# A six-layer graph network on one core: the mask fetch in four parts, layer 1's sums made in two blocks, layer 2's queries begun earlier

## The chip, the core and the metric

The kernel runs on 1 core of one Trainium2 chip. The metric is the device time of one execution in microseconds, taken as the median of several runs. Engines are named as in the profile: PE multiplies matrices, DVE and ACT work element by element, POOL does a few small things, and SP only issues DMAs, one after the other in a fixed order.

## The reference, cut to what matters

There are 3327 nodes with 256 features and one adjacency matrix `adj`, which all layers share. Layers 0, 1 and 2 are three kinds of attention; layer 3 is a projection and three graph attention layers behind each other (called 3a, 3b, 3c). Each attention is masked by `adj`:

```python
# layer 1 (3a, 3b, 3c alike)
h = x @ W
e = h @ a[:D, 0][:, None] + (h @ a[D:, 0])[None, :]
e = where(e > 0, e, slope * e)
att = softmax(where(adj > 0, e, -1e12), axis=1)
x = layernorm(x + elu(att @ h))
# layer 2
scores = (x @ Wq.T + bq) @ (x @ Wk.T + bk).T / 16
x = layernorm(x + elu(softmax(where(adj > 0, scores, -9e15)) @ (x @ Wv.T + bv)))
```

Layer 0 is an attention by cosines of the same form.

## The kernel before, in words

Nodes are cut into 26 tiles of 128 (`NT`) and the columns of the attention into 7 blocks (`NB`), six of 512 columns and a last one of 256. The main loop (L1604) goes through steps (L, b, j): layer, block, tile. "Block 1/3" below means layer 1, block 3, and "position 18" in a block means that PE is at the products of tile 18.

**Weights.** `make(s)` builds the masked weights of a step some steps ahead of the products: 3 steps for layers 0 and 2, up to 7 for the others (L1625 to L1637). A weight is one ACT instruction (L788) and one DVE instruction (L801) that multiplies by the 0/1 mask. The mask of a block is one byte an element in SBUF, 26 slices of 512. Two mask buffers exist (`mpool`, L60). Layer 0 computes all masks and stores them to `mask_d` (L1145). From layer 1 on, the mask of the next block comes back by `fetch_mask` (L423): one DMA of 1664 KB, traced in step j = 8 (L1727).

**Products and sums.** Most blocks use a Strassen-like scheme (`products`, L915): for two tiles (a pair p, 13 pairs in a block) 7 products in place of 8, 28 matmul instructions of about 0.11 us. It needs sums of the value tiles (`combine`, L833: a small POOL memset, four DVE operations on 128x128 and a store of 256 KB to `t_d`), made once for each layer and pair, and fetched again for each block and pair (`fetch_tsum`, L863, 256.5 KB). Both take a buffer with the tag "tsum", of which there are 3: so the fetch for pair p can only be issued when PE has finished pair p - 3. Layer 1's first and last block (1/0 and 1/6) use plain products (L1700) and fetch nothing. Layer 1's twelve first sums were made in block 0/6 (pairs 0 to 2, steps 6, 12, 18), block 1/0 (pairs 3 to 8, steps 1, 5, ..., 21) and block 1/1 (pairs 9 to 11, steps 1, 5, 9).

**What sets the order.** Outside of its first steps the program is ordered by a planner: instructions are sorted onto their engines when their inputs and buffers are there in the planner's own estimate of the time; the order in which they are traced is their priority. So a DMA traced in step 8 may be placed on SP's queue far earlier. `tc.issue_after(ins)` ties an instruction behind another one on its engine. At run time each queue keeps the order that the planner gave it, so that what stands behind a waiting instruction starts late with it.

**Ends of blocks.** `finish` (L1079) joins a block's products, normalizes (L1163), turns tiles by a transposing DMA (`turn`, L1002, issued at L1009; copies to `pT` at L1020), projects (L1212), and in layer 1 writes the result rows back (`v<-o`, L1293), which wait for ACT (L1275). In block 1/6 the turned features of blocks 0 to 3 come back from DRAM (`turned_again`, L1023, copies at L1034), and `block2(0)` (L534) makes layer 2's first queries: eight matmuls (L541), two ACT instructions into `gT` (L548), a maximum on DVE (L556 to L561), a tiny matmul (L564) and a dozen tiny DVE operations up to `off` (L572). It was begun in step 14 (`begin`, L1741).

Of the kernel before, what the change touches and what calls it, by code (L numbers as in the profile page):

```python
# [33 lines left out]
def gnn_stack(ctx: ExitStack, tc: tile.TileContext, a: dict, N: int, out: bass.AP):  # L34
# [8 lines left out]
    nc = tc.nc  # L43
    NT = (N + P - 1) // P
    NP = NT * P
    NB = (NP + CH - 1) // CH
# [3 lines left out]
    def bw(b):  # L50
        return min(CH, NP - b * CH)
# [41 lines left out]
    for k in range(4):  # L93
# [5 lines left out]
    V = [  # L99
        [big.tile([P, D + 1], F32, name=f"v{i}_{t}") for t in range(NT)]  # L100
        for i in range(2)
    ]
# [5 lines left out]
    mask_d = [dram.tile([P, NT * bw(b)], U8, name=f"mask_d{b}") for b in range(NB)]  # L108
# [305 lines left out]
    masks = {}  # L414

    def new_mask(b):
        return mpool.tile([P, NT * CH], U8, tag="mask", name="mask")
# [2 lines left out]
        wd = bw(b)  # L420
        return masks[b][:, j * wd : (j + n) * wd]

    def fetch_mask(b):  # L423
        m = new_mask(b)
        nc.sync.dma_start(m[:, : NT * bw(b)], mask_d[b])
        return m

    adj_sum = {}
    stages = {}
# [403 lines left out]
    def combine(key, p, v, e=None):  # L833


        b1, b2 = v[2 * p], v[2 * p + 1]
        b11, b12, b21, b22 = b1[:, H:D], b1[:, :H], b2[:, H:D], b2[:, :H]
        if key == "2" and (key, p) not in kept:
            t = wts.tile([P, 4 * H], F32, tag=("w_l0_wqk", "row_1")[p % 2], name="tsum")
        elif (key, p) in kept or key in ("0", "1"):  # L840
            t = work.tile([P, 4 * H + 1], F32, tag="tsum", name="tsums", bufs=3)
        else:
            t = work.tile([P, 4 * H + 1], F32, tag="x4k", name="tsum", bufs=2)
        if (key, p) in kept:
            tsums[kept[key, p], p] = t
        t2, t3, t4, t1 = (t[:, c : c + H] for c in range(0, 4 * H, H))
        if e is None:
            if key != "2" or (key, p) in kept:
                nc.gpsimd.memset(t[:, 4 * H :], 1.0)
            nc.vector.tensor_tensor(t1, b12, b11, ALU.subtract)  # L850
            nc.vector.tensor_tensor(t3, b22, b12, ALU.subtract)
        else:
            one = t[:, 4 * H :]
            nc.vector.tensor_scalar(one, e[:, :1], 0.0, None, ALU.is_ge)
            nc.vector.scalar_tensor_tensor(t1, b12, one, b11, ALU.mult, ALU.subtract)
            nc.vector.scalar_tensor_tensor(t3, b22, one, b12, ALU.mult, ALU.subtract)
        nc.vector.tensor_tensor(t2, b22, t1, ALU.subtract)
        nc.vector.tensor_tensor(t4, t2, b21, ALU.subtract)
        nc.sync.dma_start(t_d[key][p][:, : t.shape[1]], t)

    fetched = [None]
# [742 lines left out]
    for s, (L, b, j) in enumerate(steps):  # L1604
        last = L.key == "3c"
# [118 lines left out]
        if L.key == "0" and b < NB - 1:  # L1724
            if j == 8:
                masks[b + 1] = new_mask(b + 1)
        elif j == 8 and not (last and b == NB - 1):  # L1727
            nb = (b + 1) % NB
            masks[nb] = fetch_mask(nb)
        if (b, j) == (1, 0):  # L1730

            if L.key == "3a":
# [5 lines left out]
        nl, nb = (L, b + 1)  # L1738
        if nb == NB:
            nl, nb = (None if last else layers[L.i + 1]), 0  # L1740
        begin = 14  # L1741
        if L.is_gat and b < NB - 1:
            begin = 2 if last and b == NB - 2 else 10
        if L.key == "0" and b == 3 and j < NT // 2 - 1:
            nc.sync.dma_start(t_d["2"][j][:, 4 * H :], ones[:, :1])
        if L.key == "0" and b == NB - 1 and j % 6 == 0 and 0 < j < 24:
            combine("1", j // 6 - 1, V[1])
        if L.key == "1" and j % 4 == 1 and j < (24, 12, 0, 0, 0, 0, 0)[b]:
            combine("1", (3 if b == 0 else 9) + j // 4, V[1])
        if L.key == "1" and b == NB - 1 and j > 0:  # L1750
            if j in (2, 4, 7, 10):
                again.append(turned_again(j // 3))
# [103 lines left out]
```

## Time and profile before

| | |
|---|---|
| median of 3 runs | 2266.18 us (2260.41 to 2271.84) |
| the profiled execution's own time | 2264.42 us |
| its span, first to last instruction | 2262.6 us |
| granted TensorE clock, mean | 0.996 |
| PE busy | 2221.0 us, 98% |
| DVE busy | 2022.4 us, 89% |
| ACT busy | 1368.2 us, 60% |
| mean DMA rate | 141 GB/s |

The profiled execution is one run; 1.82 us of its time lie outside of the span. With PE busy for 98%, a reader looks for the few places where PE has nothing to do, and compares blocks of one kind with each other: every block of layers 3a to 3c with 512 columns has the same products, and those without an interruption take 44.10 to 44.21 us.

### The profile page before, as it was taken

How to read it: one execution, taken by the hardware profiler on the slowest of the kernel's cores; microseconds unless marked ns; L12 is line 12 of the kernel's file. 1: busy time of each engine (PE TensorE's matmuls, PEld its weight loads, DVE VectorE, ACT ScalarE, POOL GpSimd, SP SyncE). 2: the span in 40 equal slices, each digit the busy share in tenths (PEclk: the TensorE clock that was granted, in tenths of full speed). 3: DMA queues.
4: the chain of work that ended last, by engine and by line, in shares of the span. 5: the costliest groups of instructions: out<-in, count | busy, mean ns of one | idle time of the engine just before them, and what ended most of it. 6: DMA issues, size and time to landing. Idle time of an engine off the chain costs nothing. (4 is left out here: it accounts for less than half of the span.)

```text
span 2262.6 us, 43919 instructions
## 1 busy us (share of the span) xinstructions
PE 2221.0 (98%) x16053; PEld 2035.4 (90%) x16053; DVE 2022.4 (89%) x5482; ACT 1368.2 (60%) x2317; POOL 87.9 (4%) x257
## 2 busy tenths in 40 slices
PE   9999999999999999999999999999999999999997
PEld 7788888889999789999999999999999999899997
DVE  7789999988989688998988889999899998899997
ACT  4677777775676645455454446666666765666663
POOL 0000001000000000000000000000000000000000
PEclk9999999999999999999999999999999999999999
DMA  8655655645765622233133254556545656355542
GB/s 278 197 167 181 194 191 192 191 133 162 178 171 144 195 52 78 67 82 92 48 96 81 66 145 153 152 152 163 140 123 152 152 149 163 101 165 161 152 121 57
DMA packets 218764, 318.84 MB, mean 141 GB/s; under 512 B 97597, under 2 KB 127028, under 8 KB 213940
## 3 DMA queue, kind: packets, MB, share of 16 engines
q1 hardware_dynamic: 209636, 307.90, 47.1%
q0 software_dynamic: 8640, 7.87, 2.4%
q8 instruction: 127, 2.08, 0.4%
q14 instruction: 89, 0.73, 0.1%
q10 hardware_dynamic: 272, 0.26, 0.0%
HBM read 243.97 MB, written 40.54 MB: 126 GB/s over the span
## 5 line engine op out<-in xcount | busy, mean ns | idle before, releaser
L788 ACT ACTIVATE re<-u,nrh,th 128x512 f32<-128x512 f32 (+1 forms) x728 | 531.0, 776 | 191.8 <-DVE ft L801 156.0
L947 PE MATMUL po<-tsums,qsum 128*128 128x128 f32 (+1 forms) x3240 | 451.9, 275 | 9.8 <-DMA tsums<-t_d 7.4
L801 DVE SCALAR_TENSOR_TENSOR ft<-re,rh,mask 128x512 f32<-128x512 f32 x598 | 433.3, 742 | 14.7 <-ACT re L788 13.0
L947 PEld LDWEIGHTS po<-tsums,qsum 128*128 128x128 f32 x3240 | 405.5, 192 | 12.2 <-DMA tsums<-t_d 6.0
L947 PE MATMUL po<-v,ft 128*128 128x129 f32 x2392 | 365.3, 275 | 0.7 <-DVE ft L801 0.6
L947 PE MATMUL po<-tsums,ssum 128*128 128x128 f32 (+1 forms) x2142 | 328.4, 276 | 8.5 <-DMA tsums<-t_d 3.2
L947 PEld LDWEIGHTS po<-v,ft 128*128 128x128 f32 x2392 | 321.4, 192 | 5.8 <-DVE ft L801 1.0
L947 PEld LDWEIGHTS po<-tsums,ssum 128*128 128x128 f32 x2142 | 296.4, 192 | 24.6 <-issue 5.0
L947 PEld LDWEIGHTS po<-v,e 128*128 128x128 f32 x1196 | 169.3, 191 | 35.6 <-issue 23.7
L1700 PE MATMUL po<-v,e 128*128 128x257 f32 x832 | 192.5, 382 | 0.8 <-DVE e L525 0.8
L524 ACT ACTIVATE ex<-ps,rq 128x512 f32<-128x512 f32 (+1 forms) x183 | 118.7, 652 | 112.0 <-PE ps L511 109.2
L1700 PEld LDWEIGHTS po<-v,e 128*128 128x128 f32 x832 | 156.3, 190 | 33.4 <-issue 9.7
L947 PE MATMUL po<-tsums,ft 128*128 128x128 f32 x1196 | 183.0, 275 | 0.0
L947 PE MATMUL po<-v,e 128*128 128x129 f32 x1196 | 182.3, 275 | 0.0
L511 PE MATMUL ps<-ft 128*128 128x512 f32 (+1 forms) x364 | 167.1, 564 | 0.4 <-ACT ex L524 0.4
L947 PE MATMUL po<-v,qsum 128*128 128x128 f32 x1080 | 164.9, 275 | 0.0
L947 PEld LDWEIGHTS po<-tsums,ft 128*128 128x128 f32 x1196 | 158.0, 192 | 0.2
L496 DVE SCALAR_TENSOR_TENSOR e<-ex,mask 128x512 f32<-128x512 f32 (+1 forms) x182 | 118.2, 651 | 42.2 <-ACT ex L676 16.5
L947 PEld LDWEIGHTS po<-v,qsum 128*128 128x128 f32 x1080 | 142.3, 192 | 0.0
L525 DVE SCALAR_TENSOR_TENSOR e<-ex,mask 128x512 f32<-128x512 f32 (+1 forms) x183 | 116.0, 642 | 28.4 <-ACT ex L524 27.9
L465 DVE CUSTOM_DVE_ANT_0 acc<-acc,stage 128x1024 uint16<-128x1024 uint16 (+1 forms) x168 | 108.5, 646 | 12.6 <-DMA stage<-in_adj_a 10.6
L649 PE MATMUL ps<-gsums,ksum 128*128 128x256 f32 x408 | 112.1, 382 | 0.7 <-ACT ex L660 0.7
(330 smaller groups left out, 3751.0 us busy)
## 6 DMA issues: line engine op xcount, KB each, us to landing
tsums<-t_d SPq DMA_DIRECT2D x217, 256.5 KB
mask<-mask_d SPq DMA_DIRECT2D x30, 1664.0 KB
stage<-in_adj_a SPq DMA_DIRECT2D x78, 512.0 KB
tsums<-t3a_d SPq DMA_DIRECT2D x77, 256.5 KB
tsums<-t3b_d SPq DMA_DIRECT2D x77, 256.5 KB
tsums<-t3c_d SPq DMA_DIRECT2D x77, 256.5 KB
mask_d<-mask SPq DMA_DIRECT2D x6, 1664.0 KB
xsum<-v POOLq DMA_DIRECT2D x60, 128.0 KB, 4.1
```

What stands on the lines that cost most here:

```text
L465: nc.vector.tensor_tensor(acc, acc, st[:, h * wd : (h + 1) * wd], ALU.add)
L496: last_masked[0] = nc.vector.scalar_tensor_tensor(e[:, :wd], t_[:, :wd], 0.0, mask(b, j), ALU.add, ALU.mult)
L511: nc.tensor.matmul(ps[:, :wd], FT[j // 4][:, 0, (j % 4) * P : (j % 4 + 1) * P], FT[b][:, 1, :wd], start=True, stop=True,)
L524: nc.scalar.activation(t_[:, c], ps[:, c], AF.Exp, scale=rq[:, j : j + 1])
L525: nc.vector.scalar_tensor_tensor(e[:, c], t_[:, c], 0.0, mask(b, j)[:, c], ALU.add, ALU.mult)
L649: nc.tensor.matmul(out, l, r, start=first, stop=True, skip_group_check=True)
L788: a_ = nc.scalar.activation(t_[:, :wd], self.u[b][:, :wd], AF.Relu, bias=self.nrh[:, j : j + 1], scale=self.th[:, j : j + 1],)
L801: v_ = nc.vector.scalar_tensor_tensor(e[:, :wd], t_[:, :wd], self.rh[:, j : j + 1], mask(b, j), ALU.add, ALU.mult,)
L947: nc.tensor.matmul(o, x, y, start=(p == 0 and g not in banks[:i]), stop=(p == NT // 2 - 1 and g not in banks[i + 1 :]),)
L1700: nc.tensor.matmul(pos[k], e[:, k * P : (k + 1) * P], V[L.i % 2][i], start=(i == 0), stop=(i == NT - 1),)
```

## The change

Three edits. The mask of the next block is fetched in four DMAs (tiles 0 to 7, 8 to 13, 14 to 19, 20 to 25), traced in steps 6, 8, 10 and 12, each tied on SP behind the last fetch of sums that has been traced by then. Layer 1's sums for pairs 0 to 7 are made in block 1/0 (steps 1, 4, ..., 22) and for pairs 8 to 11 in block 1/1 (steps 1, 3, 5, 7); none in block 0/6. In block 1/6, `block2(0)` is begun in step 11 in place of 14.

```diff
-    def fetch_mask(b):
-        m = new_mask(b)
-        nc.sync.dma_start(m[:, : NT * bw(b)], mask_d[b])
-        return m
+    PARTS = (0, 8, 14, 20, NT)
+
+    def fetch_mask(b, i):
+        c = slice(PARTS[i] * bw(b), PARTS[i + 1] * bw(b))
+        with tc.issue_after(fetched[0].ins):
+            nc.sync.dma_start(masks[b][:, c], mask_d[b][:, c])
...
-        elif j == 8 and not (last and b == NB - 1):
+        elif j in (6, 8, 10, 12) and not (last and b == NB - 1):
             nb = (b + 1) % NB
-            masks[nb] = fetch_mask(nb)
+            if j == 6:
+                masks[nb] = new_mask(nb)
+            fetch_mask(nb, j // 2 - 3)
...
+        if L.key == "1" and b == NB - 1:
+            begin = 11
...
-        if L.key == "0" and b == NB - 1 and j % 6 == 0 and 0 < j < 24:
-            combine("1", j // 6 - 1, V[1])
-        if L.key == "1" and j % 4 == 1 and j < (24, 12, 0, 0, 0, 0, 0)[b]:
-            combine("1", (3 if b == 0 else 9) + j // 4, V[1])
+        if L.key == "1" and b == 0 and j % 3 == 1 and j < 24:
+            combine("1", j // 3, V[1])
+        if L.key == "1" and b == 1 and j % 2 and j < 8:
+            combine("1", 8 + j // 2, V[1])
```

## The prediction

> **What bounds the kernel now.** I read the page's busy times first, then PE's waits by stretch, then a table of blocks, then the timelines of SP and PE around each wait. The page says that PE has almost no time to give away:
>
> ```profile
> PE 2221.0 (98%) x16053; PEld 2035.4 (90%) x16053; DVE 2022.4 (89%) x5482; ACT 1368.2 (60%) x2317; POOL 87.9 (4%) x257
> ```
>
> So the whole gain lies in 2262.6 - 2221.0 = 41.6 us, some 13 of them at the ends of the span. PE's waits, of the whole run (us in total, times, longest), show what the middle holds:
>
> ```profile
> PE po L947 <- DMA tsums<-t_d: 10.5, 8, 2.3
> PE pproj L1212 <- DVE pT L1020: 3.5, 4, 2.0
> PE po L947 <- DMA tsums<-t3b_d: 2.6, 4, 1.2
> ```
>
> The first row is all of layer 1. With the same rows of t3a_d (1.0) and t3c_d (0.9), fetched sums that come late cost 10.5 + 2.6 + 1.0 + 0.9 = 15.0 us. Now blocks against each other (stretch, length, busy times, granted clock, DMA share): 1/3, 1/4, 1/6, 3b/1, 3b/2.
>
> ```profile
> 606.81:656.34 49.53, 46.34 (x383) 45.44 (x381) 43.03 (x104) 31.12 (x46) 2.91 (x4) 0.97 0.74 182
> 656.34:700.44 44.10, 44.10 (x383) 43.69 (x381) 42.20 (x98) 29.96 (x45) 3.45 (x4) 1.00 0.64 156
> ...
> 750.21:791.76 41.55, 38.71 (x149) 28.61 (x148) 27.70 (x93) 30.23 (x47) 2.58 (x3) 0.96 0.61 173
> ...
> 1702.04:1747.73 45.69, 44.47 (x383) 43.84 (x382) 42.86 (x101) 28.99 (x45) 3.67 (x6) 1.00 0.62 159
> 1747.73:1791.94 44.21, 44.21 (x383) 43.77 (x382) 42.27 (x97) 29.36 (x45) 3.64 (x6) 1.00 0.61 159
> ```
>
> Equal work takes 44.1 us undisturbed and up to 49.5 us disturbed; DVE, at 42 to 43, is close behind. Block 1/3 loses 5.43 us, more than its waits, and its clock is 0.97: see below. What disturbs is seen on SP's and then PE's timeline of 3b/1:
>
> ```profile
> 1735.93 0.32 SPq L425 DMA_DIRECT2D mask<-mask_d  x1
> 1736.51 0.32 SPq L865 DMA_DIRECT2D tsums<-t3b_d  x1
> ```
> ```profile
> 1745.18 1.16 PE L947 MATMUL po<-tsums,ssum 128*128 128x128 f32 x8 [1.22 <-DMA tsums<-t3b_d]
> ```
>
> The mask fetch sits at position 18 to 20 of nearly every block, not where step 8 would put it: the planner has pulled it up to where its buffer comes free, and there SP waits for DVE's last masked weight of the block (in 3a/2 that ended at 1484.05, and the DMA went out at 1484.08). So it is fetched a block and a half ahead, in one piece, just before the fetches for the last pairs. In the trace's packets the mask issued at 736.67 moves from 737.63 to 742.78, and the fetch issued behind it at 737.10 has its first packet at 742.29: the pieces of one DMA stand in line before those of the next. The fetch at 1736.51 thus served PE 8.7 us later. A fetch is asked for when pair p - 3 is done, two pairs, 4 positions or about 6.3 us, ahead; a mask in front takes 5 of them. Two such waits in layer 1:
>
> ```profile
> 642.10 0.32 SPq L425 DMA_DIRECT2D mask<-mask_d  x1
> 646.81 2.03 SPq L1293 DMA_DIRECT2D v<-o  x2
> 648.95 0.53 SPq L865 DMA_DIRECT2D tsums<-t_d  x1
> ```
> ```profile
> 652.27 2.05 PE L947 MATMUL po<-tsums,ssum 128*128 128x128 f32 x8 [2.28 <-DMA tsums<-t_d]
> ...
> 744.97 1.61 PE L947 MATMUL po<-tsums,qsum 128*128 128x128 f32 x12 [1.85 <-DMA tsums<-t_d]
> ...
> 764.48 3.60 PE L1212 MATMUL pproj<-w_l_w,pT 128*128 128x256 f32 x8 [1.97 <-DVE pT L1020]
> ```
>
> **The change, part by part.**
>
> **Masks in layers 3a to 3c.** The ties put part i behind the fetch for pairs 6, 7, 8 and about 9 or 10 (step 6 looks 7 ahead, to tile 12), issued at positions 8 to 16, where SP has little else. The buffer has been free for half a block, so SP waits for nothing new. The first part lands some 8 positions before DVE needs it; the last, tiles 20 to 25, a block before. The parts for the first block of the next layer are tied only to the last fetch of block 5 and may still go together at position 20, but then behind it. I take the lengths above 44.21 (3a, 3b) and 44.10 (3c): 3b/1 1.48, 3b/3 0.48, 3b/5 1.02, 3c/1 1.16; and the bare waits of blocks that also lose elsewhere, 3a/0 0.45, 3a/2 0.57, 3b/0 0.42. Sum 5.6 us. Block 3a/0 has DVE busy for 44.96 of 45.48 us, so its share may stay: I count **-5.0**.
>
> **Masks in layer 1.** Late sums at the end of 1/2 (0.91), 1/3 and 1/5 (1.85) have a mask ahead. That of 1/3 costs more than its 2.28: the granted clock then stands at 0.5 for 3.41 us (652.07 to 655.48), 13 matmuls at 0.21 in place of 0.11. Block 1/3 lost 5.43, of which 0.51 and 0.40 are two waits at its start: 4.5 for this one. The Trainium skill, "TensorE: Matmul & The Clock Gate", Part 1, says that half clock follows an idle window of about 3.4 us; here 2.28 and 1.97 us sufficed, twice, while 2.06 at 705.63 did not. By the page the removal of this wait would be worth 2.3, by the rows 4.5. Sum 0.9 + 4.5 + 1.9 = 7.3. The result rows (L1293), which wait for ACT until 646.81, stay ahead of that fetch if the planner keeps its order; without the mask the fetch still has to leave at about 647.8 and be there at 650. I count **-6.0**. The waits at block starts (1.55 at 563.7; 0.99 and 2.06 after 701) follow a transposing DMA whose issue holds SP for 4.07 us at 699.30; they have no mask ahead, and I leave them.
>
> **Queries sooner.** In block 1/6 PE stands 1.97 us for pT, then runs eight projections at half clock (0.425 in place of 0.216, 1.67 lost), then 0.87 for L564: 4.5 us. The eight matmuls of L541 (3.44 us at 0.43 each) now come three steps sooner. They read FT of block 0, whose copies end at 759.70 in ACT's timeline, before PE stands still at 762.51. If they go in front of the projections, the wait is filled and the clock stays up. The `gT` buffer shares its tag with the transposed tiles still in flight until about 762, so ACT may hold it back: **-3.0**, ends 0 and -4.5. ACT's two instructions and DVE's maximum move with it into ACT's idle 2.54 us before 764.66.
>
> **Layer 1's sums.** A sum is 4 DVE operations of 0.28 us, a store, a buffer. Three leave block 0/6, where DVE is busy 32.48 of 35.57 us and PE waits 1.2 us for weights. But the trace has nine stores of sums from 428 to 469: the planner pulls them up wherever DVE seems free, whatever step traces them, and will again; I count 0 (ends 0 and -1.7). What does change is block 1/1: four sums in steps 1 to 7 in place of three in 1 to 9, through the 3 buffers that the fetches use. Walking through, pairs 4 to 6 get their buffers 2 positions (3.1 us) before need in place of 4, and a fetch takes 2 to 3 us. Today's 1/1 does as much without loss (44.10). I count **+1.5**; ends 0 and +8, if SP waits 2.8 us (25.0 over 9, SP's waits on L858 here) at each sum.
>
> **Price of the parts.** Three more issues of 0.32 us on SP for each of 35 masks, which is idle then; packets of 13312 B take 498 ns, of 4096 B 159 ns, of 2052 B 85 ns: one of 4096 B and three of 3072 B cost at worst, at the rate of the smallest, 540 ns, 8% or 0.4 us of 5 more on the ring. DVE waits at four slices in place of one, in its lead of 7 steps. **0**, ends 0 and +1.
>
> Sum -5.0 - 6.0 - 3.0 + 1.5 = -12.5: 2264.42 becomes 2251.9. The profiled run lies 1.76 below the median of 2266.18, so I say **2253** for the median.
>
> **The rivals.** 0.5% of the median, about what a measurement of this kernel can tell from no change, is 11.3 us; the forecast is just beyond it.
>
> *The queue's order, not the mask (22%).* If the result rows and transposing DMAs of layer 1 make its fetches late anyway, and the projections stay ahead of L541, only 5.0 and 0.9 of L564 remain, some -3 to -9: 2257 to 2263. For it speaks that 1/2 and 1/5 also wait where no mask is near.
>
> *More than the forecast (10%).* With the mask gone the planner sets the last two fetches ahead of the result rows; the block starts (4.6) and 0/6 go too: all ends together give -5.6 - 7.3 - 4.5 - 4.6 - 1.7 = -23.7, about 2242.
>
> *Slower: the buffers of sums in 1/1 (7%).* The fetch of a pair waits for a sum, the sum for DVE, and SP stands at its store, 5.2 us at the longest. It decides once fetches are asked for under 2 us ahead: four such stores of 5.2 and two half clocks of 1.7 are 24 us, so -14 + 24 = +10: 2276. Against it: 1/1 today.
>
> *Slower: each DMA's start (3%).* If the ring stood still for the 0.96 us from issue to the first packet, three more for each of the 28 masks outside of layer 2 would be up to 80 us: near 2330. The packets at 742.29, right behind the mask's, speak against it. The Trainium skill, "DMA: Bandwidth & Descriptors", Rules for kernel authors, asks for 1 MiB or more in a DMA and gives a fixed cost of about 2 us; by it this edit would be a loss.
>
> **Chances.** Forecast 58% (own range 2246 to 2259; 47 of the 58 beyond 0.5%), so faster 47 + 10 = 57%, within 0.5% 11 + 22 = 33%, slower 10%. From 2243 to 2264 about 18% is left out.
>
> **What would show it.** Mask DMAs at positions 8 to 16 without a wait of SP; 3b/1, 3b/5 and 3c/1 at 44.1 to 44.3 us; 1/3 near 45; no half clock at 652 and 764; L541 ahead of L1212 in 1/6; 1/1 not above 46. I am wrong if the late sums stay with the mask gone, or if 1/1 grows.

## The result and the profile after

| | before | after |
|---|---|---|
| median | 2264.02 us (14 runs) | 2257.11 us (14 runs) |
| ratio after to before, 95% interval | | 0.9969 (0.9958 to 0.9980) |
| the profiled execution's own time | 2264.42 us | 2257.03 us |
| its span | 2262.6 us | 2255.2 us |

The change takes about 7 us, 0.31%: the sign of the forecast, but little more than half of its 12.5 us, and no longer beyond the 0.5%. The median of 2257.11 us lies inside the forecast's own range of 2246 to 2259. Lines from L425 on have moved: L425 is now L428, all others of this text stand 2 further down (L947 is L949, L1009 is L1011, L1212 is L1214). In the kernels of the experiments the shift is 0 to 3 lines.

The page's line of busy times of the changed kernel shows PE's work as before, a little shorter, and DVE's unchanged:

```profile
PE 2217.7 (98%) x16053; PEld 2031.6 (90%) x16053; DVE 2023.2 (90%) x5482; ACT 1367.6 (61%) x2317; POOL 90.9 (4%) x257
```

PE's waits in the changed kernel (us in total, times, longest) give the story in three rows:

```profile
PE pproj L1214 <- DVE pT L1022: 7.9, 4, 5.5
PE po L949 <- DMA tsums<-t_d: 4.0, 4, 1.7
PE po L949 <- DVE p L989: 2.2, 1, 2.2
```

The wait for layer 1's fetched sums fell from 10.5 to 4.0 us, and the rows of t3a_d, t3b_d and t3c_d (4.5 us together) have left the list. But the wait for `pT`, 3.5 us before with 2.0 as its longest, is 7.9 with one of 5.5. Four blocks of the changed kernel (stretch, length, busy times of PE, PEld, DVE, ACT and POOL, granted clock, DMA share, GB/s): 1/1, 1/3, 1/6 and 3b/1.

```profile
516.97:563.06 46.09, 44.36 (x381) 43.76 (x380) 39.05 (x102) 26.76 (x39) 2.35 (x5) 1.00 0.56 158
609.22:653.88 44.66, 44.34 (x383) 43.76 (x382) 41.99 (x96) 30.17 (x44) 3.42 (x4) 1.00 0.72 182
745.44:790.88 45.44, 39.42 (x148) 28.46 (x147) 27.28 (x92) 30.59 (x47) 2.49 (x2) 0.92 0.60 166
1699.17:1743.38 44.21, 44.21 (x383) 43.77 (x382) 42.34 (x97) 29.23 (x45) 3.67 (x6) 1.00 0.62 159
```

1/3 fell from 49.53 to 44.66 us and 3b/1 from 45.69 to the undisturbed 44.21. 1/1 rose from 44.10 to 46.09, and 1/6, which was to fall, rose from 41.55 to 45.44 with its clock at 0.92. SP's timeline in 3b/1 shows the parts where they were put, each right behind a fetch and without a wait:

```profile
1711.80 0.42 SPq L428 DMA_DIRECT2D mask<-mask_d  x1
1714.55 0.32 SPq L867 DMA_DIRECT2D tsums<-t3b_d  x1
1714.91 1.64 SPq L428 DMA_DIRECT2D mask<-mask_d  x1
1717.68 0.32 SPq L867 DMA_DIRECT2D tsums<-t3b_d  x1
1718.36 0.32 SPq L428 DMA_DIRECT2D mask<-mask_d  x1
```

**Where 1/6 lost.** SP's and then PE's timeline of the changed kernel around the start of 1/6 (745.44):

```profile
742.04 4.42 SPq L1011 DMA_TRANSPOSE turned<-planes  x1
746.52 0.73 SPq L428 DMA_DIRECT2D mask<-mask_d  x1
747.34 0.40 SPq L1031 DMA_DIRECT2D ft<-tr_d  x1
747.80 2.22 SPq L428 DMA_DIRECT2D mask<-mask_d  x3
750.06 1.66 SPq L867 DMA_DIRECT2D tsums<-t_d  x3
752.24 6.93 SPq L1011 DMA_TRANSPOSE turned<-planes  x1
```
```profile
757.57 1.13 PE L1702 MATMUL po<-v,e 128*128 128x257 f32 x4 [0.55 <-DVE e L803]
764.17 2.08 PE L1214 MATMUL pproj<-w_l_w,pT 128*128 128x256 f32 x4 [5.46 <-DVE pT L1022]
766.04 3.21 PE L543 MATMUL pgq<-ft,G 128*128 128x512 f32 x4
```

And SP's timeline of the kernel before, at the same place (1/6 starts at 750.21 there):

```profile
756.30 3.51 SPq L1009 DMA_TRANSPOSE turned<-planes  x1
```

The four parts of the mask for layer 2's first block go out in 1/6, and the transposing DMA that makes `pT` stands behind them: its issue holds SP for 6.93 us in place of 3.51. In the kernel before, the mask had left at 736.67, in block 1/5. PE waits 5.46 us for `pT` and then runs at half clock: four of L543 take 3.21 us in place of 1.88. L543 did not go ahead of the projections: four of it stand behind the first four of L1214, and so on.

By stretches of the two profiled executions (us, after less before): layer 0 up to 0/5 +0.3; 0/6, 1/0 and 1/1 +3.0; 1/2 to 1/5 -8.1; 1/6 +3.9; layer 2 +0.5; layers 3a to 3c -7.0. The sum is -7.4, as are the spans.

### The profile page after: what moved, and what is told of

It is laid out like the page before. It is cut to its first block, busy times and chain, and to the rows that moved or that the text cites. A ratio compares the mean times of both kernels' runs of the same rounds, so it can differ in the third digit from the quotient of the medians.

```text
span 2255.2 us, 44098 instructions
## 1 busy us (share of the span) xinstructions
PE 2217.7 (98%) x16053; PEld 2031.6 (90%) x16053; DVE 2023.2 (90%) x5482; ACT 1367.6 (61%) x2317; POOL 90.9 (4%) x257
## 5 line engine op out<-in xcount | busy, mean ns | idle before, releaser
L949 PE MATMUL po<-tsums,qsum 128*128 128x128 f32 (+1 forms) x3240 | 452.1, 275 | 7.3 <-DMA tsums<-t_d 4.0
L949 PEld LDWEIGHTS po<-tsums,qsum 128*128 128x128 f32 x3240 | 405.8, 192 | 9.2 <-issue 4.8
L949 PE MATMUL po<-v,ft 128*128 128x129 f32 x2392 | 365.7, 275 | 0.2
L949 PE MATMUL po<-tsums,ssum 128*128 128x128 f32 (+1 forms) x2142 | 327.0, 275 | 2.4 <-DVE ssum L895 1.7
L949 PEld LDWEIGHTS po<-v,ft 128*128 128x128 f32 x2392 | 321.4, 192 | 5.0 <-DVE ft L803 0.3
L949 PEld LDWEIGHTS po<-tsums,ssum 128*128 128x128 f32 x2142 | 295.5, 192 | 17.5 <-issue 5.0
L949 PEld LDWEIGHTS po<-v,e 128*128 128x128 f32 x1196 | 169.4, 191 | 35.7 <-issue 23.7
L1702 PEld LDWEIGHTS po<-v,e 128*128 128x128 f32 x832 | 155.8, 190 | 35.6 <-issue 9.7
L949 PE MATMUL po<-tsums,ft 128*128 128x128 f32 x1196 | 183.0, 275 | 0.0
L949 PE MATMUL po<-v,e 128*128 128x129 f32 x1196 | 182.5, 275 | 0.0
L949 PE MATMUL po<-v,qsum 128*128 128x128 f32 x1080 | 165.0, 275 | 0.0
L949 PEld LDWEIGHTS po<-tsums,ft 128*128 128x128 f32 x1196 | 157.9, 192 | 0.2
L949 PEld LDWEIGHTS po<-v,qsum 128*128 128x128 f32 x1080 | 142.3, 192 | 0.1
```

What stands on the lines that cost most here:

```text
L949: nc.tensor.matmul(o, x, y, start=(p == 0 and g not in banks[:i]), stop=(p == NT // 2 - 1 and g not in banks[i + 1 :]),)
L1702: nc.tensor.matmul(pos[k], e[:, k * P : (k + 1) * P], V[L.i % 2][i], start=(i == 0), stop=(i == NT - 1),)
```

## The experiments

Each kernel was timed beside runs of the kernel before (medians of 2260.77 to 2267.57 us), so the ratios are what is compared, not the medians of different rows. Lengths are those of one profiled execution, in us. "Late" is everything from 3a/0 on; "parts" in the column of 1/6 says that layer 2's first mask goes out there ahead of the transposing DMA.

| kernel | median | ratio (95% interval) | 1/1 | 1/2 to 1/5 | 1/6 | late |
|---|---|---|---|---|---|---|
| before | 2264.02 | 1 | 44.10 | 190.5 | 41.55 | 903.9 |
| the change | 2257.11 | 0.9969 (0.9958, 0.9980) | 46.09 | 182.4 | 45.44 parts | 896.9 |
| the change again, e10 | 2257.29 | 0.9966 (0.9953, 0.9979) | 45.59 | 189.4 | 44.53 parts | 898.4 |
| masks only, e1 | 2253.50 | 0.9960 (0.9946, 0.9973) | 44.10 | 180.3 | 44.27 parts | 897.8 |
| queries only, e2 | 2260.92 | 0.9998 (0.9985, 1.0011) | 44.10 | 194.9 | 40.02 | 902.0 |
| sums only, e3 | 2263.11 | 1.0008 (0.9993, 1.0024) | 44.84 | 191.3 | 41.50 | 905.9 |
| all but sums, e11 | 2255.72 | 0.9949 (0.9929, 0.9968) | 44.10 | 186.4 | 44.41 parts | 897.8 |
| all but queries, e12 | 2257.22 | 0.9958 (0.9944, 0.9973) | 45.56 | 187.8 | 44.11 parts | 896.7 |
| change, first mask late, e4 | 2251.85 | 0.9957 (0.9938, 0.9975) | 45.40 | 187.0 | 42.22 | 896.8 |
| masks only, whole and tied, e5 | 2252.44 | 0.9958 (0.9945, 0.9971) | 44.10 | 182.4 | 45.67 one piece | 898.4 |
| masks only, parts untied, e6 | 2257.84 | 0.9988 (0.9974, 1.0002) | 44.10 | 190.6 | 43.35 two parts | 899.1 |
| masks, first late, e7 | 2249.44 | 0.9949 (0.9931, 0.9967) | 44.10 | 181.3 | 40.48 | 897.6 |
| e7 and queries, e8 | 2247.33 | 0.9941 (0.9921, 0.9961) | 44.10 | 180.3 | 43.14 | 896.4 |
| e8, masks whole, e9 | 2248.48 | 0.9930 (0.9908, 0.9951) | 44.10 | 182.2 | 39.96 | 897.1 |

**Which edit does what?** The theory after the result: tying the masks brings the whole gain, and the loss in 1/6 comes from the same edit, because the parts of layer 2's first mask go out ahead of the transposing DMA. The rival: the queries, the other edit that touches 1/6, made it long. Each edit was made alone.

Masks only: the hunks of `PARTS`, `fetch_mask` and steps 6 to 12.

> Only the mask edit. Theory A (in block 1/6 the four parts of layer 2's first mask now stand in the DMA line ahead of the transposing DMA that PE waits for): 1/6 loses 8 to 9 us as in the changed kernel, against 5.0 before, and the late layers gain their 7; the whole is 8 to 9 us faster than before. Theory B (the earlier queries lengthen 1/6, since two groups of L541 stand between the projections): 1/6 loses 5 us as before, the whole is 12 to 13 us faster. Under both, 1/1 stays at 44.1 us.

Measured 0.9960 (0.9946 to 0.9973): 9 us by the ratio, as much as the whole change or more (the intervals overlap), with 1/6 at 44.27. SP's and PE's timeline of this kernel in 1/6:

```profile
745.35 6.37 SPq L1011 DMA_TRANSPOSE turned<-planes  x1
```
```profile
756.70 3.78 PE L1214 MATMUL pproj<-w_l_w,pT 128*128 128x256 f32 x8 [5.14 <-DVE pT L1022]
```

The wait and the long issue are there without the queries. Queries only (`begin = 11` in block 1/6):

> Only the earlier queries. Theory A: 1/6 loses no more than before (4 to 5 us), since the transposed tiles come as before and only the wait of 0.87 us for L564 goes; the whole within 1 us of before. Theory B: 1/6 loses 8 to 9 us, the whole is 3 to 4 us slower than before.

No difference that the runs can tell (0.9985 to 1.0011). The profile shows a small gain in its place, 1/6 at 40.02 in place of 41.55. PE's timeline there:

```profile
767.28 1.13 PE L1212 MATMUL pproj<-w_l_w,pT 128*128 128x256 f32 x4 [1.83 <-DVE pT L1020]
768.25 1.88 PE L541 MATMUL pgq<-ft,G 128*128 128x512 f32 x4
```

The wait of 1.83 us stays, since the planner puts the first projections ahead of L541 here too; only the half clock does not follow (1.88 for four is full speed). One profile can't tell whether that is the edit's doing. Sums only:

> Only the sums of layer 1 moved. If the three buffers are the cost: 1/1 takes about 46 us in place of 44.1 and 0/6 about 36.4 in place of 35.6, the rest as before; the whole 2 to 3 us slower than before. If the 2 us of 1/1 in the changed kernel came from the mask parts between its fetches: 1/1 at 44.1, the whole as before.

0.9993 to 1.0024: between 1.6 us gained and 5.4 lost. 1/1 is 0.74 us longer, and 0/6 is 0.4 shorter. That is neither of the two values expected for 1/1 (46 and 44.1): the edit alone costs less there than the 2.0 us of the changed kernel.

**The place in 1/6.** The changed kernel with layer 2's first mask traced in steps 12 to 15 of block 1/6 and tied behind the last fetch that follows the transposing DMA:

```diff
-        with tc.issue_after(fetched[0].ins):
+        with tc.issue_after(behind_[0].ins if b == 0 and behind_[0] else fetched[0].ins):
...
-        nc.sync.dma_start(tr.rearrange("p k i -> p (k i)"), tr_d[g])
+        behind_[0] = nc.sync.dma_start(tr.rearrange("p k i -> p (k i)"), tr_d[g])
...
+        elif L.key == "1" and b == NB - 1:
+            if j == 12:
+                masks[0] = new_mask(0)
+            if 12 <= j < 16:
+                fetch_mask(0, j - 12)
```

> The changed kernel, but the four parts of layer 2's first mask are traced in steps 12 to 15 of block 1/6 and tied behind the last DMA that brings turned tiles back, so that they stand behind the transposing DMA. Theory A: pT comes some 5 us sooner, 1/6 loses 3 to 5 us in place of 9.0, the whole is 11 to 12 us faster than before. Theory B: 1/6 stays at 8 to 9 us, the whole stays 7 us faster than before.

1/6 falls from 45.44 to 42.22. SP's and PE's timeline of this kernel:

```profile
753.16 2.84 SPq L1012 DMA_TRANSPOSE turned<-planes  x1
...
757.64 2.32 SPq L429 DMA_DIRECT2D mask<-mask_d  x4
```
```profile
759.90 1.13 PE L1215 MATMUL pproj<-w_l_w,pT 128*128 128x256 f32 x4 [0.53 <-DVE pT L1023]
```

With the parts behind it, the transposing DMA holds SP for 2.84 us, and the wait for `pT` is 0.53. The ratio falls by 0.0012 (2.7 us), which is within the two intervals, and the 9.7 us below the kernel before fall short of the 11 to 12 expected. Two more comparisons with and without mask data ahead (e1 and e7, e11 and e8) lower the ratio by 0.0011 and 0.0008, again within the intervals; but all 14 profiles agree. With mask data ahead the transposing issue takes 5.09 to 7.57 us (seven executions); without, 1.81 to 3.71 (seven). 1/6 lasts 44.74 us in the mean of the six with a full mask ahead, and 41.27 in that of the seven with none.

**Place or size of a piece?** The theory is that only the place on the queue counts; the rival is that the pieces must be small as well. The masks edit alone, with one piece of 1664 KB in step 8, tied behind the last fetch:

```diff
     def fetch_mask(b):
         m = new_mask(b)
-        nc.sync.dma_start(m[:, : NT * bw(b)], mask_d[b])
+        with tc.issue_after(fetched[0].ins):
+            nc.sync.dma_start(m[:, : NT * bw(b)], mask_d[b])
```

> The mask stays one DMA of 1664 KB, traced in step 8 as before, but tied behind the last fetch of sums: so it goes out at about position 10, right behind a fetch and 3.1 us ahead of the next. Theory P (the place does it: behind a fetch, away from the stores, rows and transposes of a block's end): the waits for sums in layers 3a to 3c go as in the changed kernel, 3b/1, 3b/5 and 3c/1 at 44.1 to 44.2 us, the whole 6 to 9 us faster than before. Theory S (the size does it: 5 us of one DMA in line make the next fetch late wherever it stands): a wait of 0.5 to 1.5 us now stands at positions 12 to 14 of many blocks of these layers, the whole no more than 3 us faster or slower.

0.9958 (0.9945 to 0.9971), beside 0.9960 of the four parts: the same. Two lines of SP's timeline show that its transposing DMA in 1/6 pays as well (PE's longest wait there is 3.62 us for DVE's weights: DVE waits for ACT, and ACT 5.26 us for a fetch of turned tiles that also stands behind the mask; the wait for `pT` that follows is 0.66):

```profile
742.85 0.93 SPq L426 DMA_DIRECT2D mask<-mask_d  x1
...
748.18 7.57 SPq L1010 DMA_TRANSPOSE turned<-planes  x1
```

And the four parts without the tie:

```diff
-        with tc.issue_after(fetched[0].ins):
-            nc.sync.dma_start(masks[b][:, c], mask_d[b][:, c])
+        nc.sync.dma_start(masks[b][:, c], mask_d[b][:, c])
```

> Four parts as in the mask edit, alone, but not tied: the planner pulls them up to where the mask's buffer comes free, so that they go out at positions 19 to 25, three of them side by side. Theory P: the waits of before stay (0.3 to 1.5 us in 3b/1, 3b/5, 3c/1), the whole within 3 us of before. Theory S: these waits go, the whole 6 to 9 us faster than before.

0.9988 (0.9974 to 1.0002). SP's timeline in 1/3 and a row of PE's waits of this kernel show why: the planner pulls the parts up to where the buffer comes free, in front of the block's last fetches, where the whole mask stood before.

```profile
642.29 0.80 SPq L427 DMA_DIRECT2D mask<-mask_d  x2
643.18 0.38 SPq L866 DMA_DIRECT2D tsums<-t_d  x1
643.60 0.43 SPq L427 DMA_DIRECT2D mask<-mask_d  x1
```
```profile
PE po L948 <- DMA tsums<-t_d: 6.5, 4, 3.0
```

Layer 1 keeps its loss (190.6 in this profile). The late layers gain by the size alone, 899.1 in place of 903.9. There the expectation of the place theory failed: 3b/1, 3b/5 and 3c/1 did not keep their waits (44.21, 44.21 and 44.10 us), although the parts go out at positions 19 to 22 of 3b/1. So over the whole kernel and in layer 1 the tie does the work, not the number of pieces: the intervals of the tied kernels (0.9946 to 0.9973 and 0.9945 to 0.9971) don't touch that of this one. In the late layers either brings most of the gain.

**The best of it.** Masks as changed, but layer 2's first one late, with the sums left as they were, without and with the queries:

> Only the mask edit, with the four parts of layer 2's first mask behind the transposing DMA of block 1/6 as in the run with the first mask late. If the parts in line ahead of that DMA are the cost of 1/6: 1/6 at 41 to 42 us in place of 44.3, the whole 2 to 3 us faster than the mask edit alone and 10 to 12 us faster than before. If 1/6 only trades that wait for another: 1/6 at 43.5 or more, the whole as with the mask edit alone.

> The same with the earlier queries as well, so the changed kernel without the move of layer 1's sums and with the first mask late. If the sums in 1/1 cost 1 to 2 us and the earlier queries gain 1.5 us once pT comes in time: 1/1 at 44.1, 1/6 at 40 to 41, the whole 12 to 13 us faster than before, the fastest of all. If the queries collide with the late mask in 1/6 (their chain over DVE then ends last, as the wait for L566 of 2.2 us in the run with the first mask late): 1/6 at 42 or more, the whole no faster than without them.

0.9949 (0.9931 to 0.9967) and 0.9941 (0.9921 to 0.9961): the queries add a step that the runs can't tell from nothing, and in this profiled execution 1/6 is even the longer with them (43.14 against 40.48). The last one once more with whole masks, beside the changed kernel on the same chip:

> The fastest version so far (four tied parts, layer 2's first mask late, queries sooner, sums left alone), but with each mask in one piece of 1664 KB again. If only the place counts, it gives the same ratio to the kernel before as the four parts did (0.994, some 2247 us, within 3 us) and 1/6 lasts 40 to 43 us. If the size of a piece counts as well, late sums come back behind the whole masks in layer 1 (1/2 to 1/5 above 45.5 us in the mean) and it stands 4 us or more above that version, at 2251 us or more.

> The changed kernel itself, unaltered, on the chip of this call, as the yardstick for the versions. It should repeat its ratio of 0.997 to the kernel before, 5 to 8 us below it, with block 1/6 at 44 to 47 us and a wait for pT of 4 us or more in it. If 1/6 is short here and the ratio the same, the loss in 1/6 was an accident of one execution and not the place of the mask's parts.

0.9930 (0.9908 to 0.9951) against 0.9966 (0.9953 to 0.9979): 2248.48 against 2257.29 us, with intervals that don't touch. This is faster than both kernels, and one piece is enough. In the profile of e9, 1/6 (first fence) is at full clock, and its transposing DMA holds SP for 2.00 us, ahead of the mask:

```profile
741.70:781.66 39.96, 37.05 (x149) 27.42 (x148) 27.30 (x92) 30.16 (x47) 2.58 (x3) 1.00 0.68 188
```
```profile
747.79 2.00 SPq L1012 DMA_TRANSPOSE turned<-planes  x1
...
752.09 0.82 SPq L428 DMA_DIRECT2D mask<-mask_d  x1
```

The changed kernel's second profile repeats its loss in 1/6 (a wait for `pT` of 5.12 us), so that was no accident; but 1/2 to 1/5 last 189.4 us here and 182.4 in the first, so a single profile of these blocks says little within 7 us. About half of that, 3.7 us, lies in 1/4 (50.2 against 46.5): PE waits at its start 3.04 us for the join on DVE in place of 2.17, and a spell of half clock follows (657.48 to 664.30).

**What the other two edits cost.** The changed kernel without one of them:

> The changed kernel without its sums edit: layer 1's sums are made as before, the masks in four tied parts and the queries sooner stay. Theory S (the sums edit costs more than the 1.5 us of block 1/1 that the prediction gave it, because blocks 1/2 to 1/5 also get longer with it): ratio to the kernel before of 0.995 or less, some 4 us below the changed kernel; 1/1 at 44.1 us and 1/2 to 1/5 together at 180 to 183 us. Rival (the sums cost 1.5 us in 1/1 and nothing else): ratio 0.9955 to 0.9965, 1 to 2 us below the changed kernel, 1/2 to 1/5 together anywhere between 180 and 190 us. Both expect 1/6 at 43.5 us or more, with its wait for pT.

> The changed kernel with the queries of layer 2 begun in step 14 of block 1/6 as before; masks and sums as changed. If the queries made 1/6 long, 1/6 falls to 42 us or less and the ratio to 0.995. If the parts of the mask ahead of the transposing DMA did, as the versions with only the masks and with a late first mask say, 1/6 stays at 44 us or more with a wait for pT of 4 us or more, and the ratio is 0.997 to 0.998, between the same time and 2 us above the changed kernel.

Without the queries 1/6 still has its wait, which settles that they didn't cause it. PE's timeline of e12:

```profile
766.76 3.78 PE L1214 MATMUL pproj<-w_l_w,pT 128*128 128x256 f32 x8 [4.99 <-DVE pT L1022]
```

Its ratio of 0.9958, below the 0.997 expected, shows no gain from the queries in this surrounding. Without the sums 1/1 is undisturbed, in the windows of e11:

```profile
516.26:560.36 44.10, 44.10 (x382) 43.68 (x380) 37.99 (x98) 26.95 (x39) 2.01 (x4) 1.00 0.57 161
```

The ratio of 0.9949 is where the theory of the larger cost put it, but its other mark failed: 1/2 to 1/5 took 186.4 us, not 180 to 183. Whether the sums edit lengthens those blocks stays open.

## Why the prediction was right in sign and wrong in size

The time lies inside the forecast's range, but partly by luck: the mask terms brought 4.1 us more than counted. At their forecast size, with the loss in 1/6 as it was, the median would have been some 2261 us, outside of 2246 to 2259. (The sum of the prediction gives 2253.7 us for the median; it was put down as 2253.)

**Masks in layers 3a to 3c: right, somewhat small.** Parts at positions 7 to 13 of 3b/1 without a wait of SP, 3b/1 and 3b/5 at 44.21, 3c/1 at 44.10, as said. Predicted -5.0, measured -7.0 in the first profile; the ten kernels with tied masks lie at 896.4 to 898.4, the three with the mask as before at 902.0 to 905.9, a difference of 6.5 in the mean. The share of 3a/0, which was left out because DVE is busy there, came too (45.48 to 44.74).

**Masks in layer 1: right.** Predicted -6.0, measured -8.1. The ten tied kernels take 180.3 to 189.4 us for 1/2 to 1/5 (mean 184.0), the four others 190.5 to 194.9 (191.8): -7.9. The half clock at 652 is gone in the first profile. A wait at the start of 1/4 (2.17 for DVE at 656.88, the third row of the waits) has come in its place, and in the second profile it is 3.04 us and brings the half clock back; 1/4 lasts 44.8 to 50.2 us in the ten tied kernels, 44.10 in the kernel before: without the late fetch, the join of the block before is what PE meets next. The prediction had not named what would be late next there.

**Price of the parts: right, 0.** Four parts and one piece give the same time twice (0.9960 and 0.9958; 0.9941 and 0.9930, intervals overlapping). The Trainium skill's rule for the most bandwidth is 1 MiB or more in a DMA ("DMA: Bandwidth & Descriptors", Rules for kernel authors); parts of 384 to 512 KB fall short of it, but no run here shows a loss of time.

**Layer 1's sums: right in size.** Predicted +1.5. 1/1 is 0.7 to 2.0 us longer in the five kernels with the edit, 1.4 in the mean, with waits for fetches as described (1.73 at 535.16). The edit alone costs 0.74, with tied masks 1.30 to 1.99: parts of the mask then go out between the fetches of 1/1 (531.60 and 532.72 in the changed kernel), which the term did not count; no run tests that they are the reason. The prediction contradicts itself here: it counts +1.5 in 1/1 and calls itself wrong "if 1/1 grows". 46.09 is also just beyond its own mark, "not above 46". 0/6 is no shorter, as said (35.6 in the mean of those five, 35.7 of the others). Four comparisons with and without the edit give ratios higher by 0.0008, 0.0016, 0.0018 and lower by 0.0002, 2.3 us in the mean (the changed kernel counts with the mean of its two ratios); each is within its intervals.

**Queries sooner, -3.0: the step that failed**, in two ways. First, "if they go in front of the projections, the wait is filled": they didn't. The planner kept four projections ahead of L541, in every kernel with this edit, so the wait for `pT` was not filled. Its sign "no half clock at 652 and 764" failed with it: 761.87 to 768.70 is at half clock. Four comparisons with and without the edit give ratios that differ by -0.0002, +0.0010, -0.0011 and -0.0008: 0.6 us gained in the mean, nothing that the runs tell from zero.

Second, and larger, the sentence on the masks that "the parts for the first block of the next layer are tied only to the last fetch of block 5 and may still go together at position 20, but then behind it". It was priced at nothing. In 3a/5 and 3b/5 that is what happened (positions 21 to 23), at a price of 0.9 us at most (3a/6 lasts 27.69 us after 26.82; 26.79 in e9). In layer 1 the last block has no fetches, its own transposing DMA is issued 6 us into 1/6, and the tie, which holds the mask back from block 1/5, puts it right ahead of that DMA. The price is some 3.5 us in 1/6 (44.74 against 41.27), with the wait for `pT` of 5.46 us and a half clock that the prediction wanted to remove. The prediction had looked at SP's queue for the fetches that a mask delays, not for the transposing DMA, though its own trace had such DMAs holding SP for 3.51 us (in 1/6) and 4.07.

So 1/6 gave +3.9 in place of -3.0, 6.9 us of the difference; 1/1 with its neighbours 1.5 and the rest (layers 0 and 2) 0.8; the two mask terms gave 4.1 back. -12.5 + 6.9 + 1.5 + 0.8 - 4.1 = -7.4, the difference of the spans.

**The rivals.** The time also lies, at the very edge, in the interval of "the queue's order, not the mask" (2257 to 2263), and one of its two conditions came true, the projections ahead of L541. The other did not: with the mask out of their way PE's waits for the fetches of layer 1 fell from 10.5 us to 4.0 (6.7 in the second profile), and 1.73 of the 4.0 lie in 1/1, where the sums edit costs. Neither slower rival showed: 1/1 lost 1.4 us in the mean, not 24, and three more issues for each mask cost nothing.

**Open.** What holds the transposing DMA on SP is inferred from what stands ahead of it; no kernel measured it with masks of several sizes. And what moves the waits at the starts of 1/2 to 1/5 from one execution of a kernel to the next, by 7 us in all, is not known.

## What to carry to other kernels

A transfer with much slack should be tied to its place on the queue: a planner that sees only buffers will pull it up in front of something urgent, and cutting it into pieces without the tie helped here in layers 3a to 3c, but not in layer 1. But a tie moves it behind something and so ahead of something else: go through the queue to the next urgent instruction in every block, the first and last of a layer above all, where the pattern of the others ends. And an instruction moved sooner in the trace fills a wait only if the planner also places it there.

## What the runs showed of the hardware

The issue of a transposing DMA holds SP for longer with more data in line ahead of it. In block 1/6 it took 1.81 to 3.71 us with no mask ahead (seven executions), 5.09 us with two parts of a mask, and 5.10 to 7.57 with a whole mask of 1664 KB (six). A mask is not the only cause: in the kernel before, the one at 699.30, behind result rows and stores of sums, took 4.07 us, and the one at 793.70, with no other DMA issued from SP in the 3.3 us before it, 1.23. A plain DMA of the mask or of a part of it takes 0.3 to 2.5 us of SP.

The granted clock of 0.5 comes in spells of 3.41 us or two or three times that: 3.41 us twice in the kernel before, 6.83 in the changed kernel (761.87 to 768.70, begun within the wait of 5.46 us that ends at 764.17), 10.24 in e5 (the one at the end of each trace is left out here). The Trainium skill, "TensorE: Matmul & The Clock Gate", Part 1, gives a window of 3413 ns that runs freely, and the lengths of the spells agree with it. So do their starts: within an execution they lie whole multiples of 3.41 us apart, 33 of them between 652.07 and 764.71 in the kernel before. That such a window must be idle as a whole does not agree: cut into these windows, the trace has PE busy for 39% and 42% of the two that precede the spells of the kernel before. In all 14 executions the window ahead of each of the 21 spells of layer 1 has PE busy for 45% or less, and no window of layer 1 with 47% or more was followed by a new spell. So the length of a wait alone doesn't decide: 2.71 us in e9 (until 698.19) fall into two windows with PE busy for 55% and 66%, and no spell followed; 1.86 us in e3 (until 778.62) lie in one window with 45%, and one did. The busy share is not the whole rule: seven spells of layers 3a to 3c followed windows of 51 to 72%, and what else counts no run here shows.
